# A four-layer graph network on one core: moving the statistics of one layer, and the turning of halves of two others, in a hand-written instruction order

## The chip, the cores and the metric

The kernel runs on one core of a Trainium2 chip. The metric is device time in microseconds (us) of one execution. A core has TensorE (PE, matrix products, with PEld for the loading of the stationary operand), VectorE (DVE), ScalarE (ACT), GpSimd (POOL) and SyncE (SP, which here issues nearly all DMAs). Each engine runs its own instructions in order and waits for others by semaphores.

## The reference

Input x has 32 batches of 512 nodes with 128 features in float32; adj is one 512 x 512 matrix, symmetric in its pattern. Four layers, each with layer normalisation and a ReLU ahead and a residual behind:

```python
# layer 0: softmax over the edges, two weights, diagonal apart
h = relu(layernorm(x));  A = softmax(where(adj > 0, vals, -9e15), axis=1)
x = x + (A*eye) @ (h @ W[0]) + (A*(1-eye)) @ (h @ W[1]) + bias
# layer 1: Chebyshev terms with A = adj, five of them, one weight
h = relu(layernorm(x));  x1 = adj^T @ h;  x2 = 2*adj^T @ x1 - h
x = x + relu(concat(h, x1, x2, x1, x2) @ Theta1 + bias)
# layer 2: message passing with adj*adj
h = relu(layernorm(x));  feat = relu(h @ psi_w + psi_b);  msg = (adj*adj)^T @ feat
x = x + relu(concat(msg, h) @ phi1_w + phi1_b) @ phi2_w + phi2_b
# layer 3: attention, weighted by adj
h = relu(layernorm(x));  S = tanh(((h@q) @ (h@k)^T / sqrt(128)) / 8) * 8
A = exp(S) * adj;  x = x + (A / A.sum(-1)) @ h @ v
```

For layer 3 the kernel needs adj transposed; it is turned beside layer 0 and kept in DRAM, to be loaded as `adjTx` (called the mask below) in layer 2.

## The kernel before, in words

x stays on the chip, as 16 tiles of two batches each (`xt[q]`, q = 0 to 15; a "half" m = 0 to 31 is one batch of such a tile). Products of 512 x 512 matrices with data are made in three parts: an operand is split into high, low and mid parts (`moving_parts`, L420 on ACT, L421 on POOL, L422 on DVE)[...].

**The order.** Everything inside `manual_schedule` is issued on PE, DVE, ACT and POOL in the order in which the Python code calls it, so the sequence of calls is the schedule of each engine. DMAs on SP that are wrapped in `keep_in_program_order` keep theirs too. An instruction that waits holds all behind it on its engine.

**Normalising.** `ln_stats(q)` makes the statistics of two batches: four `bn` on DVE (L245), the root `sd` on ACT (L252 in layer 2, L254 in layer 1), then `rs` and `sh` on DVE (L256, L257). The normalised and rectified `h` is made on ACT from x with `rs` and `sh`, in slices of 128 x 128 (L285 in layer 1, L1085 in `chunk` for layers 2 and 3: four for a half).

**Turning.** Features must come to the partitions. DVE transposes `h` in blocks of 32 (`hb`, L1094 in `turn_half`, one for each half), four DMAs write `hb` to DRAM (`d`, L1100), and when both halves of a q are written, one DMA reads the whole back as `hT` (`fetch`, L1108). In layer 1 the same is `turn` (with `d_hT`), after which POOL's `straighten` copies `hT` to `hs` (L974).

**Layer 1** (from 183.7 to 456.7 us) goes by pairs A = 2r and C = 2r + 1 of tiles q, r = 0 to 7. `split_up(q, b)` makes the three parts of a half of h; `first(q, b)` makes x1T = adj^T h with twelve matmuls (L405), evicted by ACT (L407); `weighed(q, b)` multiplies hs and x1T with the weights (`p_w`, 32 matmuls at L447 for the two halves of a q) and splits the result; `mix` adds it all up (L999, L1003). In each r, after `first(C, 0)`, the statistics of the tiles A - 2 and C - 2 (finished in the round before) are made for layer 2, both ahead of `first(C, 1)`. For r = 0 the steps left from layer 0 (`own`) stand there.

**Layer 2** (`layers_2_and_3`, from 456.7) goes by n = 0 to 31. Each n issues: `messages(n)` on PE; the normalising of half n + 6 (`chunk`) on ACT; the eviction `msgT` on DVE; `features(n + 2)`: p_feat on PE from hT, `feat` on DVE (L1122), its ReLU on ACT (L1123), and the three parts; `hidden(n - 1)`: two products with phi1 on PE (p_phi, L1143, L1144) and the ReLU `msgT` on ACT (L1145); `updated(n - 2)`: p_l on PE (L447), the residual x on DVE (L1153), and when a q is complete its statistics for layer 3; then the transposes of what was normalised in the same n, and the DMAs. `fetch(2, n // 2 + 3)` follows at odd n, behind the writes of d. From n = 8 on one half for layer 3 is normalised as well (`ahead_of_3`), placed after `updated`; for n = 26 to 30, where no half of layer 2 is left, two. The loads of the mask (`adjTx`) are issued at even n from 20.

**Layer 3** (from 672.5, 7.94 us for each batch) makes `key_parts`, `queries` (p_query, L1179), `scores` with tanh and exp, and `attended`. Four halves that are left are normalised and turned there, one each at n = 2 to 5.

**Buffers.** Normalised tiles (`normed_tile`, two batches each) come from a pool of three; `hb` has two; `wide_tile` (four times 512, for w, sq, keys and ex) has six.

Of the kernel before, what the change touches and what calls it, by code (L numbers as in the profile page):

```python
# [13 lines left out]
AF = mybir.ActivationFunctionType  # L14
# [15 lines left out]
def kernel(  # L30
# [181 lines left out]
    def ln_stats(q, low=False):  # L212
        for _ in stats_steps(q, low):
            pass
# [264 lines left out]
    def go(steps, n=99):  # L479
        for _ in range(n):  # L480
            if next(steps, steps) is steps:
                return
# [467 lines left out]
    def layer1(more, square):  # L950


        h, hT, hs, parts, x1, w = {}, {}, {}, {}, {}, {}
        normal, turning = {}, {}

        def normalised(q, n=2 * NT):
            if q >= NQ:
                return
            if q not in normal:
                h[q] = normed_tile(q)  # L960
                normal[q] = normed_steps(q, h[q])
            go(normal[q], n)

        def turn(q, n=3):
            if q >= NQ:
                return
            if q not in turning:
                turning[q] = turn_steps(h[q], f"hT1_{q}", hT)
            go(turning[q], n)

        def straighten(q):
            hs[q] = work.tile([P, 2, N], F32, tag="hT", name=f"hs_{q}", bufs=4)
            for b in range(2):
                nc.gpsimd.tensor_copy(split(hs[q][:, b]), hT[f"hT1_{q}"][:, :, b, :].rearrange("p b (a c) -> p a b c", c=QR))  # L974

        def split_up(q, b):
            if q < NQ:
                parts[q, b] = three(f"h_{q}_{b}")
                moving_parts(h[q][:, b].rearrange("p t f -> p (t f)"), *parts[q, b])

        def first(q, b):
            if q < NQ:
                x1[q, b] = small_tile(f"x1T_{q}_{b}")
                mixed_parts(f"x1T_{q}_{b}", adj_parts, parts[q, b], x1[q, b])

        def weighed(q, b):
            r, j = q // 2, 2 * (q % 2) + b
            if j == 0:
                w[r] = [wide_tile(f"w_{part}_{r}", F32R) for part in PARTS]
            p = projected(f"p_w_{q}_{b}", (columns(hs[q][:, b]), th[:, 1, :]), (columns(x1[q, b]), th[:, 2, :]))  # L990
            high, low, mid = (part.rearrange("p t (w f) -> p t w f", f=D)[:, :, j, :] for part in w[r])
            nc.scalar.activation(high, p, AF.Copy, scale=DOWN)
            nc.vector.tensor_sub(low, p, high.bitcast(F32))
            nc.vector.scalar_tensor_tensor(mid, p, 1.0 / UP, high.bitcast(F32), OP.mult, OP.subtract)

        def mix(r, i):
            p = bank(f"p_l1_{r}_{i}")
            for j in range(4):
                nc.tensor.matmul(p[:, blk(j)], columns(hs[2 * r + j // 2][:, j % 2])(i), th[:, 0, :],  # L999
                                 start=(j == 0), stop=False, skip_group_check=True)  # L1000
            for part in range(3):
                for t in range(NT):
                    nc.tensor.matmul(p, adj_parts[part][:, t, blk(i)], w[r][part][:, t, :],  # L1003
                                     start=False, stop=(part == 2 and t == NT - 1), skip_group_check=True)
            nc.vector.scalar_tensor_tensor(tiles(p), tiles(p), UP, spread(b1, 4), OP.mult, OP.add)  # L1005
            x = xq[r].rearrange("p w b t f -> p (w b) t f")[:, :, i, :]
            nc.vector.scalar_tensor_tensor(x, tiles(p), 0.0, x, OP.max, OP.add)

        normalised(0)
        yield  # L1010
        turn(0)
        normalised(1)
        yield
        split_up(0, 0)
        first(0, 0)
        split_up(0, 1)
        straighten(0)
        turn(1)
        for r in range(NQ // 2):
            A, C = 2 * r, 2 * r + 1  # L1020
            last = r == NQ // 2 - 1
            if r == 0:
                first(A, 1)
                split_up(C, 0)
                split_up(C, 1)
                straighten(C)
            else:
                split_up(A, 1)
                straighten(A)
                mix(r - 1, 0)  # L1030
                normalised(C, NT)
                turn(C, 1)
                mix(r - 1, 1)
                normalised(C)
                turn(C)
                mix(r - 1, 2)
                split_up(C, 0)
                go(square, r > 3)
                mix(r - 1, 3)
                split_up(C, 1)  # L1040
                first(A, 1)
            weighed(A, 0)
            weighed(A, 1)
            if last:
                more(0)
            go(square, r > 2)
            first(C, 0)
            normalised(A + 2, NT)
            if last:
                more(1)  # L1050
            for q in (A - 2, C - 2) if r else (NQ - 2, NQ - 1):
                ln_stats(q) if r else go(own[q])
            first(C, 1)
            if last:
                more(2)
            if r:
                straighten(C)
            split_up(A + 2, 0)
            normalised(A + 2)
            go(square, r > 3)  # L1060
            weighed(C, 0)
            weighed(C, 1)
            go(square, r > 3)
            turn(A + 2)
            first(A + 2, 0)
            if r == 0:
                normalised(C + 2, 0)
        more(3)
        for i in range(NT):
            mix(r, i)  # L1070
            more(4 + i)
        yield
# [3 lines left out]
    def chunk(layer, m):  # L1076


        q, b = divmod(m, 2)
        if b == 0:  # L1080
            halves_h[layer, q] = normed_tile(q)
        h = halves_h[layer, q]
        for t in range(NT):
            i = b * NT + t
            nc.scalar.activation(h[:, b, t, :], xt[q][:, b, t, :], AF.Relu,  # L1085
                                 bias=shift[q][:, i : i + 1], scale=scale[q][:, i : i + 1])

    def turn_half(layer, m):

        q, b = divmod(m, 2)  # L1090
        if b == 0:
            turned_h[layer, q] = late.tile([P, NQR, 2, NT, QR], F32, tag="hb", name=f"hb{layer}_{q}", bufs=2)
        hb = turned_h[layer, q]
        nc.vector.transpose(hb[:, :, b].rearrange("p j t r -> p t j r"),  # L1094
                            halves_h[layer, q][:, b].rearrange("p t (j c) -> p t j c", c=QR))
        if b == 1:
            d = dh[layer, q] = bounce.tile([NQR, QR, NQR, 2 * P], F32, tag=f"d{layer}", name=f"d{layer}_{q}", bufs=NQ)
            for i in range(NQR):
                tc.keep_in_program_order(
                    nc.sync.dma_start(d[:, :, i, :].rearrange("j c e -> c j e"),  # L1100
                                      hb[i * QR : (i + 1) * QR].rearrange("c j b t r -> c j (b t r)")))
# [146 lines left out]
    def layers_2_and_3():  # L1248


        later = iter(range(B))

        def ahead_of_3():
            m = next(later, None)
            if m is not None:
                chunk(3, m)
            return m

        mask_of = adjT_d.rearrange("(a b c) w -> b a c w", a=NT, c=QR)
        for n in range(B):  # L1260
            p = messages(n)
            ready = []
            if n + 6 < B:
                chunk(2, n + 6)
                ready.append((2, n + 6))
            elif n < B - 1:
                ready.append((3, ahead_of_3()))
            nc.vector.tensor_scalar(msgT[n // 4][:, n % 4], p, UP, None, OP.mult)
            biased(n)
            features(n + 2)  # L1270
            if n == B - 1:
                queries(0)
            hidden(n - 1)
            updated(n - 2)
            if 8 <= n < B - 1:
                ready.append((3, ahead_of_3()))
            for layer, m in ready:
                turn_half(layer, m)
            if n == 0:
                fetch(2, 2)  # L1280
            elif n % 2 and n + 6 < B:
                fetch(2, n // 2 + 3)
            if n in (2, 3):
                ln_stats(NQ - 4 + n)
            if n == 12:
                weights_of_3()
            if n == 20:
                adjTx.append(matrix_tile("adjTx"))
            if n >= 20 and n % 2 == 0 and n < 28:
                i = (n - 20) // 2  # L1290
                tc.keep_in_program_order(nc.sync.dma_start(adjTx[0][:, i, :], mask_of[i]))
            if n in (26, 28, 30):
# [7 lines left out]
        for n in range(B):  # L1300
# [11 lines left out]
                    continue  # L1312
            attended(n - 1)
            mapped(n + 1)
            if n >= 2:
                m = ahead_of_3()
                if m is not None:
                    turn_half(3, m)
            if n % 2 == 0:
                fetch(3, n // 2 + 3)  # L1320
        attended(B - 1, width=1)
# [95 lines left out]
```

## Time and profile before

| what | us |
|---|---|
| median of 3 runs (931.77, 932.40, 932.95) | 932.4 |
| the profiled execution | 931.7 |
| its span, first to last instruction | 929.9 |
| PE busy in it | 908.7 |
| layer 1, start to end | 183.7 to 456.7 |
| layer 2, start of n = 0 to the first query of batch 1 | 456.7 to 672.5 |
| layer 3, to the end | 672.5 to 929.9 |
| DVE, ACT, POOL busy | 660.0, 527.3, 487.5 |
| mean granted TensorE clock | 0.998 of full |

The span is what the instruction times in the profile refer to; what lies around it is 1.8 us. An engine's busy time says how much of the span it worked; a line of waits names the waiting engine, tile and line, then what released it, the total in us, the number of times and the longest.

### The profile page before, as it was taken

How to read it: one execution, taken by the hardware profiler on the slowest of the kernel's cores; microseconds unless marked ns; L12 is line 12 of the kernel's file. 1: busy time of each engine (PE TensorE's matmuls, PEld its weight loads, DVE VectorE, ACT ScalarE, POOL GpSimd, SP SyncE). 2: the span in 40 equal slices, each digit the busy share in tenths (PEclk: the TensorE clock that was granted, in tenths of full speed). 3: DMA queues.
4: the chain of work that ended last, by engine and by line, in shares of the span. 5: the costliest groups of instructions: out<-in, count | busy, mean ns of one | idle time of the engine just before them, and what ended most of it. 6: DMA issues, size and time to landing. Idle time of an engine off the chain costs nothing.

```text
span 929.9 us, 15159 instructions
## 1 busy us (share of the span) xinstructions
PE 908.7 (98%) x5432; PEld 774.0 (83%) x5433; DVE 660.0 (71%) x1348; ACT 527.3 (57%) x1156; POOL 487.5 (52%) x435
## 2 busy tenths in 40 slices
PE   8999999999999999999999989999999999999998
PEld 4899999878888888888877767676689999999998
DVE  8888885655665665566677676666888777777775
ACT  5864553342442352353546777777688666666663
POOL 5968999742132253532245444444465666655553
PEclk9999999999999999999999999999999999999999
DMA  9255643113213312303322343555513221212111
GB/s 256 61 165 173 173 116 106 46 47 91 63 38 115 81 46 68 91 24 84 108 82 70 112 117 95 141 146 153 144 30 96 74 75 57 80 57 80 59 35 46
DMA packets 83915, 86.06 MB, mean 93 GB/s; under 512 B 6784, under 2 KB 74624, under 8 KB 83840
## 3 DMA queue, kind: packets, MB, share of 16 engines
q1 hardware_dynamic: 83552, 84.57, 32.0%
q8 instruction: 43, 0.70, 0.3%
q10 hardware_dynamic: 288, 0.52, 0.2%
q14 instruction: 32, 0.26, 0.1%
HBM read 44.17 MB, written 40.89 MB: 91 GB/s over the span
## 4 chain that ended last, share of the span: by engine, by line
PE 73%; DVE 10%; ACT 8%; issue 3%; DMA 3%; SPq 2%; POOL 1%; DVEq 0%; ACTq 0%; POOLq 0%
PE p_av L1228 12%; PE p_l L1003 10%; PE p_score L1206 9%; PE p_x1T L405 7%; PE p_w L447 5%; PE p_l_c L393 4%; DVE bn L245 3%; PE p_l L999 3%; PE p_l_a L393 3%; PE p_hv L447 3%; PE p_l_d L393 3%; PE p_g L447 3%; PE p_query L1179 2%; SPq L1100 2%; DMA d<-hb 2%
## 5 line engine op out<-in xcount | busy, mean ns | idle before, releaser
L421 POOL TENSOR_TENSOR low_feat<-feat,high_feat 128x512 fp32r<-128x512 f32 x32 | 54.3, 1698 | 128.2 <-ACT high_feat L420 128.2
L1228 PEld LDWEIGHTS p_av<-hv,ex 128*128 128x128 f32 x1024 | 119.2, 191 | 2.7
L1228 PE MATMUL p_av<-hv,ex 128*128 128x129 f32 x1024 | 119.4, 274 | 0.0
L285 ACT ACTIVATE h<-x,sh,rs 128x128 f32<-128x128 f32 x256 | 102.8, 483 | 11.9 <-DVE sh L257 11.1
L428 POOL TENSOR_TENSOR key<-key 128x512 fp32r<-128x512 f32 x32 | 55.2, 1724 | 96.7 <-DVE key L427 96.7
L1201 DVE TENSOR_TENSOR ex<-ex,adjTx 128x512 f32<-128x512 f32 x64 | 72.3, 1130 | 45.9 <-ACT ex L1199 42.9
L1085 ACT ACTIVATE h<-x,sh,rs 128x128 f32<-128x128 f32 x256 | 102.8, 483 | 0.0
L1201 POOL TENSOR_TENSOR ex<-ex,adjTx 128x512 f32<-128x512 f32 x64 | 94.7, 1498 | 7.0 <-issue 4.2
L421 POOL TENSOR_TENSOR low_h<-h,high_h 128x512 fp32r<-128x512 f32 x32 | 48.2, 1515 | 78.4 <-ACT high_h L420 78.0
L407 ACT ACTIVATE x1T<-p_x1T 128x512 f32<-128x512 f32 x32 | 19.0, 592 | 122.2 <-POOL low_h L421 62.0
L245 DVE BATCH_NORM_STATS2 bn<-x 128x6 f32<-128x256 f32 x244 | 85.8, 416 | 0.0
L1199 ACT ACTIVATE ex<-ex 128x512 f32<-128x512 f32 x128 | 78.8, 650 | 0.0
L1207 ACT ACTIVATE ex<-p_score 128x512 f32<-128x512 f32 x128 | 73.8, 604 | 1.4 <-PE p_score L1206 1.1
L432 ACT ACTIVATE high_query<-p_query 128x512 fp32r<-128x512 f32 x32 | 19.1, 598 | 76.8 <-PE p_query L1179 76.8
L974 POOL COPY hs<-hT 128x512 f32<-128x512 f32 x32 | 18.7, 612 | 83.9 <-DMA hT<-d_hT 78.4
L422 DVE SCALAR_TENSOR_TENSOR mid_feat<-feat,high_feat 128x512 fp32r<-128x512 f32 x32 | 27.4, 857 | 44.6 <-ACT high_feat L420 44.6
L1005 DVE SCALAR_TENSOR_TENSOR p_l<-p_l,b 128x512 f32<-128x512 f32 x32 | 22.4, 699 | 44.5 <-PE p_l L1003 44.5
L1094 DVE STREAM_TRANSPOSE hb<-h 128x512 f32<-128x512 f32 x64 | 45.0, 705 | 12.3 <-ACT h L1085 7.8
L447 PE MATMUL p_w<-th,x1T 128*128 128x128 f32 x256 | 50.3, 278 | 1.9 <-ACT x1T L407 1.9
L447 PEld LDWEIGHTS p_l<-phi,msgT 128*128 128x128 f32 x256 | 32.9, 193 | 22.2 <-ACT msgT L1145 13.4
L1206 PE MATMUL p_score<-low_query,key 128*128 128x512 f32 x128 | 50.5, 394 | 0.0
L1206 PE MATMUL p_score<-high_query,key 128*128 128x512 f32 x128 | 50.5, 394 | 0.0
(220 smaller groups left out, 2365.7 us busy)
## 6 DMA issues: line engine op xcount, KB each, us to landing
d<-hb SPq DMA_DIRECT2D x128, 128.0 KB, 2.4
hT<-d SPq DMA_DIRECT2D x32, 512.0 KB, 3.9
d_hT<-hb_hT SPq DMA_DIRECT2D x112, 128.0 KB, 2.4
hT<-d_hT SPq DMA_DIRECT2D x28, 512.0 KB, 3.3
x<-in_x_dram SPq DMA_DIRECT2D x32, 256.0 KB, 5.9
out_dram<-x SPq DMA_DIRECT2D x31, 256.0 KB, 2.4
adjT_d<-adj_squares SPq DMA_DIRECT2D x4, 256.0 KB
adj_crossed<-in_adj_dram SPq DMA_DIRECT2D x4, 256.0 KB
```

Of the source, the lines that this page charges most:

```text
L245: nc.vector.bn_stats(st[:, k].rearrange("p e s -> p (e s)"), xt[q][:, b, t : t + 2, :].rearrange("p t f -> p f t"))
L285: nc.scalar.activation(h[:, b, t, :], xt[q][:, b, t, :], AF.Relu, bias=shift[q][:, i : i + 1], scale=scale[q][:, i : i + 1])
L393: nc.tensor.matmul(p[:, i * 2 * D : (i + 1) * 2 * D], a[:, k, blk(i)], b[:, k], start=(first and i == 0 and k == 0), stop=(k == 1), skip_g ...
L421: nc.gpsimd.tensor_sub(low, x, high.bitcast(F32))
L447: nc.tensor.matmul(p[:, blk(t)], hT(t), w, start=(i == 0), stop=(i == len(terms) - 1))
L1003: nc.tensor.matmul(p, adj_parts[part][:, t, blk(i)], w[r][part][:, t, :], start=False, stop=(part == 2 and t == NT - 1), skip_group_check= ...
L1085: nc.scalar.activation(h[:, b, t, :], xt[q][:, b, t, :], AF.Relu, bias=shift[q][:, i : i + 1], scale=scale[q][:, i : i + 1])
L1199: nc.scalar.activation(ex[:, t, :], ex[:, t, :], AF.Exp, scale=8.0)
L1201: eng.tensor_mul(split(ex[:, t, :]), split(ex[:, t, :]), crossed(mask[:, t, :]))
L1206: nc.tensor.matmul(p, keys[n][i][:, t, :], query[n][i], start=(i == 0), stop=(i == 2))
L1207: nc.scalar.activation(crossed(ex[:, t, :]), split(p), AF.Tanh, scale=UP / (8.0 * math.sqrt(D)))
L1228: nc.tensor.matmul(po[:, i, : D + 1], ex[:, t, blk(i0 + i)], hv[:, t, :], start=(t == 0), stop=(t == NT - 1))
```

## The change

In layer 1, `split_up(0, 1)` is called before `first(0, 0)` instead of after it, and the second of the two statistics of each round (tile C - 2; for r = 0 the steps `own` of the last tile) is called after `weighed(C, 1)` instead of before `first(C, 1)`.

In layer 2, halves are transposed one n later than they are normalised (`turn_ready(now)`), and before `updated(n - 2)` instead of after it. The half for layer 3 is normalised at the head of n, ahead of layer 2's, from n = 7 on, and one only for each n up to 30, so that 24 halves instead of 28 are done in layer 2. `fetch(2, n // 2 + 2)` is issued at even n. The mask is loaded at odd n. In layer 3 the eight halves left are normalised at even n from 2 to 16 and transposed at the odd n after.

The halves of layer 3 no longer lie in tiles of the normalised kind but in wide ones, four halves each.

```diff
         split_up(0, 0)
+        split_up(0, 1)
         first(0, 0)
-        split_up(0, 1)
...
             normalised(A + 2, NT)
...
-            for q in (A - 2, C - 2) if r else (NQ - 2, NQ - 1):
-                ln_stats(q) if r else go(own[q])
+            ln_stats(A - 2) if r else go(own[NQ - 2])
             first(C, 1)
...
             weighed(C, 0)
             weighed(C, 1)
+            ln_stats(C - 2) if r else go(own[NQ - 1])
             go(square, r > 3)
             turn(A + 2)
             first(A + 2, 0)
...
     def chunk(layer, m):
...
-        if b == 0:
-            halves_h[layer, q] = normed_tile(q)
-        h = halves_h[layer, q]
+        if layer == 3 and m % 4 == 0:
+            h = wide_tile(f"h3_{m}")
+            halves_h.update({(3, m + i): tiles(h[:, i]) for i in range(4)})
+        elif layer == 2 and b == 0:
+            h = normed_tile(q)
+            halves_h.update({(2, m + i): h[:, i] for i in range(2)})
+        h = halves_h[layer, m]
...
-        later = iter(range(B))
+        later, ready = iter(range(B)), []
 
         def ahead_of_3():
-            m = next(later, None)
-            if m is not None:
+            m = next(later, B)
+            if m < B:
                 chunk(3, m)
-            return m
+                ready.append((3, m))
+
+        def turn_ready(now):
+            for layer, m in now:
+                turn_half(layer, m)
...
         for n in range(B):
             p = messages(n)
-            ready = []
+            now, ready = ready, []
+            if 7 <= n < B - 1:
+                ahead_of_3()
             if n + 6 < B:
                 chunk(2, n + 6)
                 ready.append((2, n + 6))
-            elif n < B - 1:
-                ready.append((3, ahead_of_3()))
             nc.vector.tensor_scalar(msgT[n // 4][:, n % 4], p, UP, None, OP.mult)
             biased(n)
             features(n + 2)
             if n == B - 1:
                 queries(0)
             hidden(n - 1)
+            turn_ready(now)
             updated(n - 2)
-            if 8 <= n < B - 1:
-                ready.append((3, ahead_of_3()))
-            for layer, m in ready:
-                turn_half(layer, m)
             if n == 0:
                 fetch(2, 2)
-            elif n % 2 and n + 6 < B:
-                fetch(2, n // 2 + 3)
+            elif n % 2 == 0 and n + 4 < B:
+                fetch(2, n // 2 + 2)
...
-            if n >= 20 and n % 2 == 0 and n < 28:
+            if n >= 20 and n % 2 and n < 28:
...
-            if n >= 2:
-                m = ahead_of_3()
-                if m is not None:
-                    turn_half(3, m)
+            if n % 2:
+                turn_ready(ready)
+                ready = []
+            elif n:
+                ahead_of_3()
```

More of the change, by code (lines that the diff above doesn't have):

```diff
@@ L1079, in chunk @@
         q, b = divmod(m, 2)
-        if b == 0:
-            halves_h[layer, q] = normed_tile(q)
-        h = halves_h[layer, q]
+        if layer == 3 and m % 4 == 0:
[5 more added lines that the diff above has]
+        h = halves_h[layer, m]
         for t in range(NT):
             i = b * NT + t
-            nc.scalar.activation(h[:, b, t, :], xt[q][:, b, t, :], AF.Relu,
+            nc.scalar.activation(h[:, t, :], xt[q][:, b, t, :], AF.Relu,
                                  bias=shift[q][:, i : i + 1], scale=scale[q][:, i : i + 1])
@@ L1094, in turn_half @@
         nc.vector.transpose(hb[:, :, b].rearrange("p j t r -> p t j r"),
-                            halves_h[layer, q][:, b].rearrange("p t (j c) -> p t j c", c=QR))
+                            halves_h[layer, m].rearrange("p t (j c) -> p t j c", c=QR))
         if b == 1:
```

## The prediction

> **What bounds the kernel now.** I read the page first: busy time by engine, then the slices.
>
> ```profile
> PE 908.7 (98%) x5432; PEld 774.0 (83%) x5433; DVE 660.0 (71%) x1348; ACT 527.3 (57%) x1156; POOL 487.5 (52%) x435
> ...
> PE   8999999999999999999999989999999999999998
> ```
>
> TensorE is busy 908.7 of 929.9 us, and this change alters no matmul. All that an edit can win is its 21.2 us of gaps (and time lost to a lower clock). The slices (23.25 us each) show few of them, so I went to the list of what PE waited for:
>
> ```profile
> PE p_l L447 <- ACT msgT L1145: 4.3, 6, 1.4
> PE p_feat L447 <- DMA hT<-d: 2.0, 4, 0.8
> ...
> PE p_query L1179 <- POOL key L428: 2.0, 2, 1.1
> PE p_w L447 <- ACT x1T L407: 1.9, 8, 0.3
> PE p_x1T L405 <- ACT high_h L420: 1.3, 1, 1.3
> ...
> PE p_x1T L405 <- POOL low_h L421: 0.7, 1, 0.7
> ```
>
> Columns: total us, times, longest. The last three are layer 1, the first three are layer 2 and its end. Layer 1 first: eight equal waits, so I took one of them in the chain of waits (start, duration, what):
>
> ```profile
> 229.48 2.81 PE p_x1T L405 x12
> 232.31 0.60 ACT x1T L407
> 232.91 1.54 ACT h L285 x4
> 234.44 0.21 ACT sd L254
> 234.67 0.21 DVE rs L256
> 234.91 0.17 DVE sh L257
> 235.08 1.35 DVE bn L245 x4
> ...
> 236.66 0.59 ACT x1T L407
> ...
> 237.29 1.83 PE p_w L447 x14
> ```
>
> ACT evicts x1T of (C,0), normalises, and takes the first root (sd). The second sd waits until DVE has done rs, sh and four bn, and the eviction of x1T (C,1) stands behind that sd. PE gets it 0.24 us late.
>
> Layer 2 next, by the timeline of ACT and of DVE around one pair of batches (start, duration, in brackets the idle time before and its releaser):
>
> ```profile
> 551.26 0.30 ACT L252 ACTIVATE sd<-bn,eps_low 128x8 f32<-128x8 f32 x1 [2.13 <-DVE bn L245]
> 551.47 3.17 ACT L1085 ACTIVATE h<-x,sh,rs 128x128 f32<-128x128 f32 x8
> ...
> 564.72 0.30 ACT L252 ACTIVATE sd<-bn,eps_low 128x8 f32<-128x8 f32 x1 [2.12 <-DVE bn L245]
> ```
> ```profile
> 553.14 0.71 DVE L1094 STREAM_TRANSPOSE hb<-h 128x512 f32<-128x512 f32 x1 [0.52 <-ACT h L1085]
> ```
>
> From sd to sd is 13.46 us for two batches, while PE needs 6.30 per batch (messages 2.88, features 0.89, phi 2 x 0.86, p_l 0.81): 12.60. ACT and DVE, each waiting for the other, are the slower loop by 0.86 per pair once layer-3 halves run beside layer 2. Batches 13 to 29 are 10.15 us longer than 6.30 each. At the end PE waits 1.68 for the first keys and its granted clock is 0.5 for 3.41 us from 664.1 (loss 1.7).
>
> **What the skill says.** "TensorE: Matmul & The Clock Gate", Part 1, The HAM clock gate: the clock is either full or half, and is judged over free-running windows of 3413 ns. The trace agrees with the size (0.5 for 3.413 us), though PE was only partly idle there. Its table calls the ScalarE, VectorE and GpSimd queues strictly first in, first out, and lets TensorE pull weight loads ahead; the x1T lines above show the first. "GPSIMD Engine Reference", 1. Specifications: GpSimd and VectorE share SBUF interfaces and contend when DVE reads two SBUF inputs. Seen: mid_feat (DVE) took 0.69 when low_feat (POOL) followed it, and 1.82 in the 5 of 32 times when POOL went first. "DMA: Bandwidth & Descriptors", Anatomy of one DMA: a fixed 2 us is mostly the write's receipt. Here d<-hb lands 2.4 us after issue, hT<-d between 3.2 (alone) and 5.0 (beside other transfers).
>
> **The change part by part.**
>
> 1. *First split of layer 1.* high_h, mid_h and low_h of (0,1) now stand before x1T (0,0) on their engines. Before, the start of the first product to the start of the third took 4.61 + 7.28 = 11.89. Without the waits of 1.26 and 0.66 a product takes 2.8 to 3.0 and the next, with its two p_w, 6.48 (the same pair at 222.72): 9.48. **-2.4**; the excess over 1.92 is two weight loads (0.19 each), which can't be pulled ahead of operands that are not there. If POOL's low_h is still late (1.3 to 1.8 each, two in a row), -1.9.
>
> 2. *Statistics of layer 1, eight times.* The second bn, sd, rs, sh goes behind weighed (C,1). x1T (C,1) can then follow the first sd at 234.65 instead of 236.66, and is needed at 237.05: 1.8 us to spare. The product and its weights take 6.97 there and 6.48 for (A,1), where nothing waits: 0.49 x 8 = **-3.9** (0.24 is wait, 0.19 the weight load). What moved now delays turn (A+2) on DVE by some 2.2 us and x1T (A+2,0)'s eviction on ACT by 2.0. Behind the turn stand four d_hT issues on SP, the fetch, then POOL's hs copy. SP's fetch of A is queued behind C's first d_hT anyway, and hs, ready at 255.97, is used at 259.3: covered by 3.3; I take zero. If that cover failed, up to 1 us each time, which I keep in the range.
>
> 3. *Layer 2, the pair.* Halves are transposed one batch after their normalising, before x and bn on DVE. ACT's number of h stays, so by single durations: sd, rs, sh and eight h to the relu 3.6; relu to high_feat 0.66; relu of msgT 0.57 and eight h 3.1; feat 0.7; high, mid 1.3; two hb 1.25; x 0.6; bn to sd 1.46; hand-overs about 0.4: **13.64**. The 0.52 wait for h is gone, but both hb now lie ahead of bn in every pair, where before only one did. +0.18 x 9 pairs = +1.6. Layer-3 halves begin two batches earlier: one more pair at the excess of 1.04, +1.0. Batches 26 to 30 normalise one half instead of two: their excess, 1.75, goes: -1.75.
>
> 4. *The fetch.* hT of pair q is fetched one batch later, behind a transpose that is itself one batch later. In the trace, the transpose of half 9 would end at about 490.9, d is issued until 492.2, lands at 494.65 (2.4), the fetch lands at 498.0 (3.3), and p_feat wants it at 494.0: PE waits **3.9** at n = 6. After that hT is late by what the ACT loop is slow, about 1.0 each second batch, taking the place of p_l's waits, not adding. The loop hb, four d, landing, fetch, features, feat, relu, high, mid, hb is 12.07 with a landing of 3.2, below 13.64. d2 and d3 are now written in different batches, so SP no longer holds the fetch behind four d3 issues (1.75), and the waits of hb for d (0.5) go. A wait of 3.9 should bring a window at half clock, 1.7, of which the next wait (1.0) takes up 1.0: +0.7. Bounds for this part: 0 (ACT was to be late anyway) and +6.
>
> 5. *End of layer 2.* From n = 31 to layer 3 took 14.66. The same matmuls without waits and at full clock take 10.33. Keys of batch 0 now come in time, since ACT is not behind: **-4.3** (0 if ACT is still late).
>
> 6. *Layer 3.* Eight halves instead of four are normalised here: 4 x 1.55 us more on ACT and 4 x 0.62 on DVE, spread over 15 batches of 7.94 in which ACT is busy 66% and DVE 77%. PE has no wait but one there. Zero, at most +1. The halves' own tiles take a spare buffer of the wide ones; the keys' and ex's turn comes as before: zero, at most +1.
>
> Sum: -2.4 - 3.9 + 1.6 + 1.0 - 1.75 + 3.9 + 0.7 - 4.3 = **-5.15**. The profiled execution took 931.7 (span 929.9), which gives 926.55; the median of the runs, 932.4, is 0.7 above it, so **927.2**.
>
> **Rivals.**
> - *A, as summed*, 0.60: 924 to 930.
> - *B, layer 2 wins too*, 0.16. For it: DVE no longer waits for ACT's h, 0.52 per pair, and if hand-overs fall better the pair comes to 13.0 rather than 13.64, -6 over ten pairs. Against it: both hb stand before bn. **921**.
> - *C, given back in layer 2*, 0.13. POOL's low_feat gets the port first more often, since DVE's order around mid_feat changed: +1.1 at mid_feat, all on the loop. In half the pairs, +5: **932**, no difference.
> - *D, the fetch becomes the bound*, 0.11. Its loop has 12.07 + (landing - 3.2): over 13.64 from a landing of 4.8. It costs 1 us per pair and us beyond, ten pairs. Slower than before by 0.2% needs +7, a landing of 5.5; at 6, **939**. For it: 4.3 to 5.0 was measured for fetches close behind d3 writes and the loads of adjTx. Against it: these now fall in the other batch.
> - That layer 1's edits do nothing (x1T held by something else) is for part 2 excluded by (A,1), the same work at 6.48.
>
> **Numbers.** 0.2%, 1.9 us, is about what a measurement of this kernel can tell from no change: faster below 930.5, slower above 934.3. A is faster almost wholly (0.58), B wholly, C is split (0.04 faster, 0.07 same, 0.02 slower), D has 0.09 slower. Faster 0.78, same 0.11, slower 0.11. The range from 921 to 934 leaves out most of D and the end of B; A's own is 924 to 930.
>
> **What would show it.** p_w's eight waits and both p_x1T waits gone: steps 1 and 2. p_feat's wait for hT grown from 2.0 to over 10 us with one near 4 at about 490, and p_l's gone: step 4. sd to sd of 13.6 at steady state: step 3. Layer 3 begun 10.3 us after n = 31, at full clock: step 5; 7.94 per batch after it: step 6. I am wrong if sd to sd is below 13.3 or above 14.0, if landings of hT exceed 4.8, or if hs in layer 1 is waited for.

## The result, and the profile after

| | median us | runs | lowest to highest |
|---|---|---|---|
| before | 932.17 | 11 | 931.30 to 932.95 |
| after | 929.42 | 11 | 927.27 to 931.55 |

The ratio is 0.9972, with a 95% interval of 0.9962 to 0.9981: 2.6 us faster, about half of the 5.15 forecast. The times after spread over 4.3 us and follow the granted clock of each run: 0.999 in the run of 927.27, 0.998 in those up to 929.00, 0.996 in the six from 929.42 on. The profiled execution of the kernel after took 931.2 (span 929.3) and is one of these last, so its span holds more half-clock time than the one before.

The list of what PE waited for, in the kernel after (total us, times, longest):

```profile
PE p_feat L447 <- DMA hT<-d: 13.1, 10, 3.6
...
PE p_query L1183 <- POOL key L428: 1.2, 1, 1.2
PE p_x1T L405 <- DVE mid_h L422: 1.2, 1, 1.2
```

The eight waits of p_w for x1T are gone. So are both waits of p_x1T for high_h and low_h, but a new one, for mid_h, stands in their place. p_l no longer waits for msgT; p_feat waits 13.1 us for hT in its stead, where it waited 2.0. The page's rows of PE and its clock show where:

```profile
PE   8999999999999999999998999999999999999998
...
PEclk9999999999999999999998999999999999999999
```

One slice, 488 to 511 us, has both the gap and the lower clock. The windows view of the kernel after cuts it (us, then busy time of PE, PEld, DVE, ACT, POOL, then granted clock, DMA share and GB/s):

```profile
488.62:492.58 3.96, 1.10 (x5) 0.56 (x3) 3.13 (x7) 1.28 (x3) 3.09 (x3) 1.00 0.56 180
492.58:499.41 6.83, 6.07 (x16) 4.03 (x17) 3.05 (x7) 3.67 (x8) 1.83 (x3) 0.50 0.02 5
```

PE works for 1.1 of 4 us, and the next 6.83 us are at half clock. In this execution that is two windows of 3.41; before had one, at 664.

By stages: layer 1 from its first product, layer 2 from the load of its first stationary operand, the rest of layer 3 from the first query product of batch 1 (profiled executions; a second execution of the kernel after, with one half-clock window like before, is put beside it, and the experiments told of below):

| kernel | layer 1 | layer 2, to the query of batch 1 | rest of layer 3 |
|---|---|---|---|
| before | 273.0 | 215.7 | 257.4 |
| after | 267.9 | 219.9 | 257.4 |
| after, second execution (a_after) | 267.9 | 218.5 | 257.3 |
| layer 1 edits only (e1) | 267.9 | 215.6 | 257.4 |
| statistics only (e2) | 269.1 | 215.5 | 257.4 |
| layers 2 and 3 only (e3) | 273.1 | 218.4 | 257.7 |
| half 9 early (e4) | 267.4 | 215.2 | 257.3 |
| PE kept warm (e5) | 267.8 | 216.5 | 257.3 |
| low_h on DVE (e6) | 266.7 | 219.5 | 257.3 |
| halves of 3 late (e7) | 267.8 | 209.3 | 257.3 |
| e4, e6, e7 together (e8) | 266.7 | 209.6 | 257.3 |
| turned in the same n (e9) | 267.4 | 205.1 | 257.4 |
| turned behind x (e10) | 267.4 | 220.7 | 259.6 |
| e9, e7, e6 together (e12) | 266.7 | 201.2 | 257.3 |

Layer 1 gave 5.1 us, layer 2 took 2.7 (4.2 with the second window) back, layer 3 is unmoved.

### The profile page after: what moved, and what is told of

Its sections match the earlier page's. It is cut to its first block, busy times and chain, and to the rows that moved or that the text cites. A ratio compares the mean times of both kernels' runs of the same rounds, so it can differ in the third digit from the quotient of the medians.

```text
span 929.3 us, 15172 instructions
## 1 busy us (share of the span) xinstructions
PE 906.4 (98%) x5433; PEld 775.1 (83%) x5433; DVE 668.5 (72%) x1348; ACT 527.7 (57%) x1156; POOL 488.0 (53%) x435
## 4 chain that ended last, share of the span: by engine, by line
PE 80%; DVE 5%; DMA 4%; POOL 4%; ACT 4%; issue 2%; SPq 1%; DVEq 0%; POOLq 0%; ACTq 0%
PE p_av L1232 12%; PE p_l L1003 10%; PE p_x1T L405 9%; PE p_score L1210 9%; PE p_w L447 6%; PE p_msgT L1138 4%; PE p_l_c L393 3%; PE p_l L999 3%; PE p_hv L447 3%; PE p_l_d L393 2%; PE p_g L447 2%; PE p_query L1183 2%; PE p_l_a L393 2%; ACT h L1089 2%; PE p_feat L447 2%
## 5 line engine op out<-in xcount | busy, mean ns | idle before, releaser
L421 POOL TENSOR_TENSOR low_feat<-feat,high_feat 128x512 fp32r<-128x512 f32 x32 | 56.5, 1767 | 131.9 <-ACT high_feat L420 131.4
L1205 DVE TENSOR_TENSOR ex<-ex,adjTx 128x512 f32<-128x512 f32 x64 | 82.5, 1289 | 34.9 <-ACT ex L1203 33.1
L1205 POOL TENSOR_TENSOR ex<-ex,adjTx 128x512 f32<-128x512 f32 x64 | 99.4, 1572 | 7.1 <-issue 4.2
L428 POOL TENSOR_TENSOR key<-key 128x512 fp32r<-128x512 f32 x32 | 50.3, 1570 | 94.4 <-DVE key L427 41.7
L422 DVE SCALAR_TENSOR_TENSOR mid_feat<-feat,high_feat 128x512 fp32r<-128x512 f32 x32 | 24.4, 764 | 55.4 <-ACT high_feat L420 55.4
L254 ACT ACTIVATE sd<-bn,eps 128x8 f32<-128x8 f32 x46 | 13.9, 302 | 64.5 <-DVE bn L245 61.4
L1210 PE MATMUL p_score<-mid_query,key 128*128 128x512 f32 x128 | 50.4, 394 | 0.0
L447 PEld LDWEIGHTS p_feat<-psi,hT 128*128 128x128 f32 x256 | 33.4, 195 | 19.4 <-issue 11.3
```

Source lines behind the costliest of these rows:

```text
L421: nc.gpsimd.tensor_sub(low, x, high.bitcast(F32))
L447: nc.tensor.matmul(p[:, blk(t)], hT(t), w, start=(i == 0), stop=(i == len(terms) - 1))
L1205: eng.tensor_mul(split(ex[:, t, :]), split(ex[:, t, :]), crossed(mask[:, t, :]))
L1210: nc.tensor.matmul(p, keys[n][i][:, t, :], query[n][i], start=(i == 0), stop=(i == 2))
```

## The experiments

Each time is a median; before was run beside it on the same chip, and the ratio is to that.

### Layer 1 alone, and its two edits apart (e1, e2)

```diff
 # e2: the kernel before, with
-            for q in (A - 2, C - 2) if r else (NQ - 2, NQ - 1):
-                ln_stats(q) if r else go(own[q])
+            ln_stats(A - 2) if r else go(own[NQ - 2])
...
             weighed(C, 1)
+            ln_stats(C - 2) if r else go(own[NQ - 1])
 # e1: the same, and
         split_up(0, 0)
+        split_up(0, 1)
         first(0, 0)
-        split_up(0, 1)
```

> The kernel before with both edits of layer 1 and nothing else of the change. Theory (layer 1's gain is its own, as the two profiles show it: 273.0 us before, 267.9 after): 5.1 us less than before, 927.0, ratio 0.9945; the eight waits of p_w for x1T gone, one wait of p_x1T for mid_h of about 1.2 us in their place, layers 2 and 3 as before. Rival (what layer 1 wins is lost again where layer 2 begins, since its first halves are then late): 929 to 931.

> The kernel before with the second statistics of each round moved behind the weighed products of C, and nothing else. Theory: 8 x 0.5 = 4.0 us less, 928.1; the first product of layer 1 keeps its two waits (1.26 and 0.66). The difference to the run with both edits is then the first split's worth, 1.1 and not the 2.4 of the prediction. If the first split is worth 2.4, this run is 2.4 slower than that one.

Measured: e1 925.19 against 931.06, ratio 0.9940 (0.9928 to 0.9953); e2 928.98, ratio 0.9970 (0.9959 to 0.9980). The medians differ by 3.8, but four of e2's seven runs had a clock of 0.996, and none of e1's. Among the runs with full clock e1 takes 925.0 to 925.4, e2 926.8 and 926.9, before 930.1 to 930.9: 3.7 for the statistics and 1.7 for the split. The stages say 3.9 and 1.2. So the statistics are worth what the prediction said, the split half of it, and the gain of layer 1 reaches the end undiminished.

### Layers 2 and 3 alone (e3)

```diff
 # the changed kernel, with the layer 1 lines of e1 put back as before
```

> The changed kernel with layer 1 put back as before: layers 2 and 3 of the change alone. Theory (the profile after has layer 2 to the first query of batch 1 in 219.9 us, before 215.7): 2 to 4 us slower than before, 934.5, with the wait of 3.6 at n = 6, half clock behind it, and runs that spread by 3 to 4 us. Rival (the stall at n = 6 comes only with the earlier end of layer 1): no change, 932.

Measured: 934.46 against 931.06, ratio 1.0039 (1.0026 to 1.0051): 3.4 us slower by the medians. The wait of 3.6 at n = 6 is there too, so it does not come from layer 1's earlier end. The spread was 1.3 only: four of the five runs had the same clock.

### The wait at n = 6 taken away (e4)

```diff
             turn_ready(now)
+            if n == 3:
+                turn_ready(ready)
+                ready = []
             updated(n - 2)
...
+            elif n == 3:
+                fetch(2, 4)
-            elif n % 2 == 0 and n + 4 < B:
+            elif n % 2 == 0 and n + 4 < B and n != 4:
                 fetch(2, n // 2 + 2)
```

> The changed kernel, but half 9 of layer 2 is transposed at n = 3 (right after half 8, where its normalised half has long been ready) and fetched at n = 3 instead of n = 4. Theory (the wait of 3.6 at n = 6 is additional, and brings the half clock): wait and half clock gone, 5 to 6 us less than the changed kernel, 924, with runs within 1.5 us. Rival 1 (PE must come to stand behind ACT and DVE by these 3.6 us anyway; the wait only moves to n = 8 and after): half clock gone at most, 927.5 to 929. Rival 2 (it is the clock alone that varies): 927.

Measured: 926.82 against 931.06, ratio 0.9962 (0.9948 to 0.9975), runs from 925.65 to 928.35. By the ratios that is about 1 us better than the kernel after (0.9972, and 0.9975 for a_after; the intervals overlap), not 5 to 6. The wait at n = 6 is gone, but p_feat still waits 11.0 us in all, 2.0 of it at n = 8, and n = 7 to 29 take 2.1 us more than in a_after. So most of the 3.7 only moves, as rival 1 has it; the time alone would fit rival 2 as well. The clock is under full in four of five runs. Behind which waits is not seen, since the profiled run is the fifth.

### The same wait, with PE kept busy (e5)

```diff
+            if n == 6:
+                idle = bank("p_warm")
+                for _ in range(14):
+                    nc.tensor.matmul(idle, sq[0][:, 0, blk(0)], sq[0][:, 0, :], start=True, stop=True)
             features(n + 2)
```

> The changed kernel with 14 matmuls of 128x512 on data at hand (their result is not used) ahead of the features of n = 6, so that PE works through the wait of 3.6 us and its clock has no reason to fall. Theory 1 (the half clock is a loss of its own): no half clock at 493, 1.7 to 3.4 us less than the changed kernel in each run that had it, times within 1 us. Theory 2 (ACT and DVE set the pace from there on, so that what PE loses by the clock it waits less later, as the run with half 9 early suggests: its waits at n = 8 and after grew to 2.0): the clock is full, but at most 1 us is won, and p_feat's later waits grow by 2 to 3 us.

Measured: 927.09 against 931.43, ratio 0.9955 (0.9942 to 0.9967); the kernel after on the same chip (a_after) 929.05, ratio 0.9975. The PE timelines of the kernel after and of e5 (start, duration):

```profile
488.62 1.10 PE L1138 MATMUL p_msgT<-sq_mid,mid_feat 128*128 128x512 f32 x4
493.34 2.05 PE L447 MATMUL p_feat<-psi,hT 128*128 128x128 f32 x8 [3.62 <-DMA hT<-d]
```
```profile
488.83 3.37 PE L1281 MATMUL p_warm<-sq_high 128*128 128x512 f32 x14
492.54 1.13 PE L447 MATMUL p_feat<-psi,hT 128*128 128x128 f32 x8 [0.33 <-DMA hT<-d]
```

The wait for hT is filled, not shortened, and the clock is full in all five runs. n = 6 takes 10.08 us instead of 11.94 in a_after, and the later waits of p_feat stay (9.5 less the 0.3 here, against 12.9 less 3.7). Theory 1 holds for the loss: the half clock cost 1.9 for one window, on top of the wait. Its forecast of the spread does not: with the clock full the runs still lie between 926.55 and 928.69. The loss fits what the Trainium skill says in "TensorE: Matmul & The Clock Gate", Part 1, The HAM clock gate, of a clock that falls after an idle window. The places listed at the end show that about half a window of idle time was enough here.

### The new wait in layer 1 (e6)

The DVE and POOL timelines of the kernel after show what holds mid_h:

```profile
185.15 0.19 DVE L256 RECIPROCAL rs<-sd 128x8 f32<-128x8 f32 x1
185.38 1.24 DVE L257 SCALAR_TENSOR_TENSOR sh<-bn,rs 128x8 f32<-128x8 f32 x1
186.54 2.17 DVE L422 SCALAR_TENSOR_TENSOR mid_h<-h,high_h 128x512 fp32r<-128x512 f32 x2
```
```profile
184.05 2.55 POOL L421 TENSOR_TENSOR low_h<-h,high_h 128x512 fp32r<-128x512 f32 x2 [3.19 <-ACT high_h L420]
```

sh, of eight columns, takes 1.24 us, where it took 0.17 before: it ends when POOL ends its second low_h. Only then does mid_h of the first half start, with PE waiting. The operation just ahead of it, rs, also has eight columns, but one input; it ran beside POOL in 0.19.

```diff
         split_up(0, 0)
-        split_up(0, 1)
+        parts[0, 1] = high, low, mid = three("h_0_1")
+        half = h[0][:, 1].rearrange("p t f -> p (t f)")
+        nc.scalar.activation(high, half, AF.Copy, scale=DOWN)
+        nc.vector.tensor_sub(low, half, high.bitcast(F32))
+        nc.vector.scalar_tensor_tensor(mid, half, 1.0 / UP, high.bitcast(F32), OP.mult, OP.subtract)
         first(0, 0)
```

> The changed kernel, but the low part of half (0,1) in layer 1's first split is made by DVE instead of POOL. Theory (POOL's low_h of (0,1) holds the port that POOL and DVE share, DVE's sh took 1.24 us instead of 0.17 and mid_h came 1.5 us late): the wait of p_x1T for mid_h (1.2) gone, first product to second 2.8 to 2.9 instead of 4.39, 1.2 to 1.5 us less. Rival (mid_h is late because of what DVE has before it, not because of the port): wait stays within 0.3 of 1.2.

The DVE timeline of e6:

```profile
184.66 0.17 DVE L257 SCALAR_TENSOR_TENSOR sh<-bn,rs 128x8 f32<-128x8 f32 x1
184.74 0.69 DVE L422 SCALAR_TENSOR_TENSOR mid_h<-h,high_h 128x512 fp32r<-128x512 f32 x1
```

Measured: the wait is gone, first product to second is 2.96 instead of 4.39, layer 1 is 1.2 shorter. So POOL's second low_h is what held sh. That it does so through a shared port is what the Trainium skill says ("GPSIMD Engine Reference", 1. Specifications): GpSimd and VectorE share their SBUF interfaces and contend when a DVE instruction has two SBUF inputs. The trace agrees: sh has two inputs (bn and rs) and was held, rs has one and was not. The wait is not the same in every execution: in e4, e9 and e10, where POOL's next copy (hs) begins 0.3 to 0.4 later, the first mid_h takes 0.68 instead of 1.15 and PE waits 0.7 instead of 1.2. The whole run gained little: 928.79 against 931.43, ratio 0.9968 (0.9957 to 0.9980), a_after 0.9975. Five of its six runs had the clock of 0.996 (two windows) and took 928.5 to 929.2; a_after's with that clock took 929.4 to 930.4.

### Layer 3's halves moved out of layer 2 (e7), and three edits together (e8)

```diff
-            if 7 <= n < B - 1:
+            if 21 <= n < B - 1:
                 ahead_of_3()
...
 # layer 3
-            if n % 2:
-                turn_ready(ready)
-                ready = []
-            elif n:
+            turn_ready(ready)
+            ready = []
+            if n:
                 ahead_of_3()
```

> The changed kernel, but layer 3's halves are normalised in layer 2 only from n = 21 on (10 instead of 24), the other 22 in layer 3, one in each batch from n = 1, turned one batch later. Theory (beside a layer-3 half ACT, DVE and the fetch need 13.8 us for two batches and PE 12.6; in layer 3 ACT has 2.7 us to spare in each batch, a half takes 1.55): seven pairs less at an excess of 1.2, 8 us less than the changed kernel, 921; layer 3 stays at 7.94 for each batch. Rival 1 (ACT's in-order queue makes PE wait for tanh and exp in layer 3): 8.2 to 8.5 for each of 22 batches there, no gain or a loss. Rival 2 (the pairs are slow for layer 2's own halves): nothing changes.

Measured: 919.60 against 931.43, ratio 0.9867 (0.9854 to 0.9881). n = 9 to 23 take 6.3 each, and each batch of layer 3 still 7.94, though 22 of them now carry a half. The pairs were slow for the second half beside them, and layer 3 has the room.

> The changed kernel with three edits of the earlier runs together: half 9 turned and fetched at n = 3, low_h of (0,1) on DVE, layer 3's halves in layer 2 only from n = 21. Theory (with no layer-3 half beside it the loop of ACT, DVE and fetch is faster than PE, so the wait at n = 6 is now really gone and not only moved, and with it the half clock): 919.6 less 1.3 (split), 3.6 (wait) and 1.8 (clock), 913. Rival (the wait moves to n = 8 as it did in the run with half 9 alone): 917.

Measured: 919.95 against 932.12, ratio 0.9870 (0.9858 to 0.9883), no better than e7. The split's 1.2 is there, but the wait at n = 6 (3.7 in e7) is now one of 3.2 at n = 8, with the same half clock. The rival's wait came, if not its time of 917, and it came without any layer-3 half near. What is left as its cause is turning and fetching later, which e9 takes back.

### Turned in the same n (e9), and turned later but behind x (e10)

```diff
 # e9
-            now, ready = ready, []
+            ready = []
...
-            turn_ready(now)
             updated(n - 2)
+            turn_ready(ready)
+            ready = []
...
-            elif n % 2 == 0 and n + 4 < B:
-                fetch(2, n // 2 + 2)
+            elif n % 2 and n + 6 < B:
+                fetch(2, n // 2 + 3)
 # e10
-            turn_ready(now)
             updated(n - 2)
+            turn_ready(now)
```

> The changed kernel, but in layer 2 every half is transposed in the n in which it is normalised, behind updated, and fetched at odd n, as before the change; all else (layer 1, layer 3's halves ahead from n = 7, one for each n, their own tiles) stays. Theory (transposing one n later is what costs layer 2 the wait of 3.6, the half clock behind it, and makes the fetch late in each pair; the other edits of layer 2 cost about 1 and win the end's 4.3): wait and half clock gone, p_feat's waits small, p_l's back, 4 to 5 us less than the changed kernel, 924.5. Rival (the pairs with a layer-3 half are slow whichever way they are turned, the excess of 11 to 12 us in n = 8 to 29 stays and PE waits for p_l instead): 927 to 928.

> The changed kernel, but the transposes of the halves one n back stand behind updated (x, bn and the root's round trip) on DVE instead of ahead of it. Theory (hT's lateness is the pace: the fetch waits for hb, and here hb comes 0.6 to 2.6 later): pairs of 14.2 to 14.6 instead of 13.8, 4 to 8 us more than the changed kernel, 933 to 937. Rival (bn to sd on ACT is the pace, as the prediction's step 3 has it, and x and bn come 1.25 earlier here): pairs of 13.0 to 13.4, 4 us less.

Measured: e9 915.43 against 932.12, ratio 0.9820 (0.9808 to 0.9833). That is 16.7 us better than before, 9 better than the theory had it and 12 better than the rival. The DVE timeline of e9:

```profile
565.51 0.69 DVE L422 SCALAR_TENSOR_TENSOR mid_feat<-feat,high_feat 128x512 fp32r<-128x512 f32 x1 [1.36 <-ACT high_feat L420]
566.12 0.68 DVE L1157 TENSOR_TENSOR x<-p_l,x 128x512 f32<-128x512 f32 x1
566.72 1.41 DVE L245 BATCH_NORM_STATS2 bn<-x 128x6 f32<-128x256 f32 x4
568.50 0.20 DVE L256 RECIPROCAL rs<-sd 128x8 f32<-128x8 f32 x1 [0.37 <-ACT sd L252]
```

x follows mid_feat at once, bn follows x, and ACT's roots are 12.3 to 12.6 us apart from 530.6 to 605.1, where they were 13.6 to 14.2 after and, from 551 on, 13.4 to 13.8 before. PE, at 12.6, is the bound again from n = 17 to 25, and p_feat waits 1.8 us in all. What the kernel before lost is in its list of DVE's waits; the same two lines of e9 stand below:

```profile
DVE hb L1094 <- ACT h L1085: 7.8, 16, 1.1
...
DVE hb L1094 <- DMA d<-hb: 4.6, 7, 0.9
```
```profile
DVE hb L1098 <- DMA d<-hb: 3.8, 2, 2.1
...
DVE hb L1098 <- ACT h L1089: 0.2, 1, 0.2
```

In the steady state a pair of batches of the kernel before has one wait of each kind, 0.52 and 0.51. Its 13.46 less both is 12.43, which is about what e9's pairs take.

The wait for h: layer 3's half was normalised at the end of n and transposed right behind, so DVE stood for ACT, and feat behind it. In e9 that half is normalised at the head of n and transposed at its end; of 7.8 us 0.2 is left. ACT's order in the steady state is the one before had, so what has changed is that DVE takes layer 3's half a batch behind ACT. Layer 2's own half, which e9 transposes in the same n, was never late: moved one n back it only delays its fetch.

The wait for d: an `hb` is free again when its writes to d have landed. In the kernel before the second halves of both layers' pairs come in the same n, and SP issues eight writes in a row. In the change and in e9 layer 3's halves begin at n = 7 instead of 8, so that the writes of the two layers fall in different n. First SP and DVE in the kernel before, then SP in e9:

```profile
552.65 3.72 SPq L1100 DMA_DIRECT2D d<-hb  x8
558.81 0.71 DVE L1094 STREAM_TRANSPOSE hb<-h 128x512 f32<-128x512 f32 x1 [0.51 <-DMA d<-hb]
```
```profile
549.77 9.94 SPq L1104 DMA_DIRECT2D d<-hb  x8
```

What e9 still has of this wait, 3.8, comes where the mask is loaded.

e10: 932.25 against 932.12, ratio 1.0006 (0.9995 to 1.0017), and runs from 929.40 to 937.12 with a clock from 0.998 down to 0.991. The trace has pairs of 13.6 on average, a little faster than after, and keys that come 1.9 late at the start of layer 3, with a half-clock window behind them (the rest of layer 3 is 2.2 longer than after). Neither side's pairs (14.2 to 14.6, 13.0 to 13.4) came out. I read that as hT and bn being both on the loop, so that giving one way takes from the other; no run shows it apart. What the run does show is that moving the turn behind x does not by itself win back what the change costs in layer 2.

### The best of these (e12)

It is e9 with the edits of e7 and e6.

> The changed kernel with three edits of the earlier runs: halves turned in the n in which they are normalised (915.4 alone), layer 3's halves in layer 2 only from n = 21, low_h of (0,1) on DVE. Theory (each takes another loss: the first the late fetch, the second what is left of the excess at n = 12 to 16, 2 us, the third 1.3 of the first split): 912, full clock, no wait at n = 6. Rival (the first has taken the losses that the second took, and the second puts work beside the loads of the mask): 914 to 915.

Measured: 910.49 against 931.95, ratio 0.9771 (0.9757 to 0.9784), five runs between 910.46 and 910.83, all at full clock. The windows view over layer 2 of e12 (columns as above):

```profile
450.20:651.30 201.10, 201.10 (x1020) 153.35 (x1019) 139.84 (x272) 119.51 (x259) 102.26 (x99) 1.00 0.36 103
```

PE has no gap in 201 us. The edits add up better than the theory had it: with fewer halves in layer 2 the last losses of e9 (3.8 us at n = 12 to 16 and 26 to 28) are gone too, of which the theory had counted 2.

## Why the prediction was right, and where it was wrong

The direction and range held, and so did most of the mechanism; the sum was -5.15, the measured change -2.6. The faster kernel comes from layer 1 alone: layer 2, forecast to lose 1.15 in sum, lost 2.7. With a_after, whose clock is that of before's profile, the terms are:

- **Step 2, statistics**: forecast -3.9; e2's layer 1 gives -3.9. The cover named for the delayed turn held: hs is not waited for.
- **Step 1, first split**: forecast -2.4, measured -1.2 (e1 against e2). The step that failed: DVE was left out of it. I had read from the trace how POOL holds DVE (mid_feat 0.69, or longer in 5 of 32; those took 1.46 to 1.84, not 1.82 each) and did not ask which DVE work POOL's second low_h would hold. Its lower figure of -1.9, for a late low_h, did not ask it either. e6 shows the missing 1.2.
- **Step 3, the pairs**: forecast +0.85 in sum, measured +1.3 (n = 4 and n = 7 to 29 of a_after against before). sd to sd was put at 13.64; it is 13.6 and 13.9 to 14.2 in turn, mean 13.8 (single pairs pass the 14.0 that it named as its limit, the mean does not): every second pair DVE waits for p_feat, which the prediction counted as hidden. That the sum comes so close is in part luck: n = 26 to 29 won 0.9 where 1.75 was booked, n = 7 to 12 lost 3.0 where the earlier start was to cost 1.0, and n = 13 to 25 won 1.0 where the pairs were to cost 1.6.
- **Step 4, the first late fetch**: forecast 3.9 and 0.7 for the clock; n = 6 of a_after has 3.7 and, with the rest of its 5.66 us over before, 2.0. The wait was right to 0.2. That the next wait would take up 1.0 of the clock's loss was wrong: e5 shows it comes in full. In the profiled run, one of the six slowest of eleven, it comes twice; the other five have the same clock.
- **Steps 5 and 6**: forecast -4.3 and 0, measured -4.2 and -0.1.

The median of 929.42 lies in rival A's own range, near its upper end. Rival B (921) did not come, nor C (mid_feat over 1 us twice, not more often than the five times before), nor D (hT landed in 3.2 to 4.2, under the 4.8 where it would have begun to decide).

What the prediction missed is behind its sum. It booked the waits of hb for h (0.52) and for d (0.5) as the gain of turning later, and the late fetch as its price. e9 shows that gain and price are separate. The two waits go, all but the 3.8 beside the mask, although every half is turned in the n in which it is normalised. The price, 13.4 us of layer 2 (218.5 to 205.1, 1.9 of it half clock), is paid for nothing. Which edit removes which wait is argued from the timelines: the head of n for h, the start at n = 7 for d. Neither was run by itself, nor was e9's order without the change's other edits in layer 2 (one half for each n, own tiles, the mask at odd n).

Why one execution has one half-clock window and another two, the traces tell in part. In all eleven places where the clock falls in the middle of a profiled execution, PE works for 1.8 us or less of the 3.41 before. Half clock lasts a second window in three of them (after, e6, and e10 at n = 6), where the gap reaches into the first so far that PE works for 2.5 to 2.7 us of it; in the other eight it works for 2.9 or more. Two windows of a_after, the columns as above:

```profile
489.80:493.25 3.45, 0.46 (x4) 0.49 (x5) 3.04 (x9) 1.18 (x4) 2.21 (x3) 1.00 0.44 152
493.25:496.67 3.42, 3.42 (x10) 1.98 (x9) 0.90 (x3) 1.93 (x4) 0.00 (x1) 0.50 0.02 5
```

Left open is why the border of a window falls at another place of the gap from run to run, and why some runs of the kernel before have no half clock at all.

## What to carry to other kernels

When an engine waits for work just issued elsewhere, give the pair some distance, but ask first what stands behind the consumer. In a steady loop an earlier producer and a later consumer can come to the same order of the queues, as ACT's in e9 and before. Layer 3's half can be transposed a batch later for nothing, because its hT is first fetched at n = 26. Behind layer 2's half stands a round trip of 7.7 us (in the kernel after, from the transpose of half 9 at 485.5 to the landing of its hT at 493.2), with PE waiting at its end. A wait that is taken away at one place and comes back at the next belongs to a loop, and only a shorter loop, or less work in it, removes it. And before work is put earlier on POOL, see what DVE does at that moment.

## What the runs showed of the hardware

- One gap of 3.7 us on PE cost 1.9 more through the clock, in steps of one window of 3.41 us at half speed. Filled with 14 matmuls whose result is not used, it cost nothing beyond itself.
- PE did not have to be idle for a whole window. Before, the clock fell at 664.1 behind gaps of 0.52, 0.30 and 0.86 (1.7 us of work in 3.41); in e10 it fell at 679.8 behind one gap of 1.88 (1.5 us of work).
- Much of the scatter of a kernel's times followed the clock: 910.46 to 910.83 at full clock in e12, 929.40 to 937.12 in e10, where the mean clock went from 0.998 to 0.991. Not all of it: e5 spread over 2.1 us at full clock.
- A DVE operation of two inputs on eight columns took 1.24 us instead of 0.17 while POOL ran a subtraction of 128x512; one of a single input took 0.19 beside it.
- In e9 writes of d landed up to 7.2 us after issue (2.4 as a rule) in the stretch in which the mask is loaded, and hb waited 2.1 and 1.7 for them.
